# A depthwise 7x7 convolution as sixteen 32x32 tiles of TensorE, with rows cut into halves and columns into residues of four

## The chip, the core and the metric

The kernel runs on one core of one Trainium2 chip. The metric is the device time in microseconds (us) of one execution. TensorE (PE, with weight loads shown as PEld), VectorE (DVE), ScalarE (ACT) and GpSimd (POOL) compute; SyncE (SP) only issues transfers (DMA), which ScalarE and GpSimd can do as well. The core's transfers are carried out by 16 DMA engines.

## What is computed

A ConvNeXt block and a selective scan, in float32, on x of shape (32, 96, 56, 56):

```
h = depthwise 7x7 convolution of x (padding 3) + conv_b
h = (h - mean over channels) * rsqrt(var + eps) * ln_g + ln_b
h = gelu(h @ w1 + b1) @ w2 + b2           # 96 -> 384 -> 96, at every pixel
x = h * layer_scale + x
x = silu(depthwise 5x5 convolution of x + conv_b)
dts, Bs, Cs = x_proj_w @ x                # 6, 4 and 4 rows
delta = softplus(dt_w @ dts + dt_b)
P = exp(cumsum(max(delta * A, log eps)))  # over the 3136 tokens of an image
hs = P * cumsum(delta * Bs * x / max(P, eps))
y = sum over n of hs * Cs + x * Ds
```

A depthwise convolution mixes only pixels of one channel. On TensorE it becomes a product with a band matrix: input rows stand on the partitions, the weights hold the seven vertical taps of one horizontal tap, and one matmul is needed for each horizontal tap (or group of them).

## The kernel before, in words

The host lays x out as [96 channels, 112 rows, 896 columns]: 112 rows are two groups of images by 56 rows, 896 columns are 16 images by 56. Four stages follow one another, each through tensors in device memory (`conv1_d`, `block_d`, `conv2_d`, `du_d`).

**First convolution** (lines 141 to 363). A job is one channel: 80 jobs have both image groups, and the last 16 channels are done as 32 jobs of one group each, so that the first group's sums are ready early. For each job SP loads x by groups of 56 rows (`load_x`, L160) and the weights by two transfers (`taps_of`, L314, from a table written once, L184). Then the columns are split into even and odd by copies (L328 on POOL and DVE, L329 on ACT) into `xq`, the odd ones on partitions 0 to 55, the even ones on 64 to 119. That puts two horizontal taps into one contraction of 120 rows, so four matmuls with 448 columns do seven taps (L334; each is two passes, that is two matmul instructions and two weight loads). ACT evicts with the bias (L343), POOL issues the stores to `conv1_d` (L347), and DVE and ACT collect the sums for the norm over channels: difference to channel 0 (L356), its sum (L357), its square (ACT, L358), the sum of squares (L359). The preparation of the other stages' weights (`beside`) runs between jobs. `finish_norm` turns the sums of one image group into `rstd_d`.

**MLP** (L369 to L485). 28 groups of four rows. `load_rows` loads for each group the reciprocal deviation `r` (L394), three blocks of 32 channels of `h` (L399) with four rows named as the outermost dimension, and three of `x` (L404, 32 channels by one row in a transfer). DVE normalises (L411), TensorE multiplies by w1 in four row tiles (L421), ACT applies Gelu (L431), TensorE multiplies by w2 in four column tiles (L440), DVE adds the bias and x (L451, twice for each result), and POOL issues the stores to `block_d` (L463).

**Second convolution** (L492 to L579). One channel at a time: weights (L510), 120 rows by 1920 B twice (L521), four column tiles of TensorE (L533), Silu (L547), copies that interleave the columns (L556), a store of 28 rows (L562).

**Scan** (L587 to L810). 64 steps of 1568 tokens, 192 units of 32 channels by 4 states. SP loads `xs` (L621), TensorE and ACT make delta (L638, L646), POOL its product with x (L652), SP stores both (L655) and loads them spread over the states (L695). ACT makes the decay (L701 to L703), POOL multiplies by B (L707), DVE scans (L717, L720, L724), POOL multiplies by C (L735), TensorE sums over the states (L748), ACT copies and stores (L758, L759).

Instructions run on each engine in the order in which the program has them, after a scheduler has arranged what isn't pinned (`pin`). SP issues its transfers in that order too, waiting where a buffer isn't free. The lines that the change and the prediction's steps touch:

Of the kernel before, what the change touches and what calls it, by code (L numbers as in the profile page):

```python
# [15 lines left out]
B2, BI = 2, 16  # L16
# [7 lines left out]
WP = 128  # L24
W2 = W // 2
MP = 64
P1 = (K1 + 1) // 2
# [3 lines left out]
RW = 32  # L31
QP = QW + 1
# [6 lines left out]
EPS = 1e-9  # L39
APART = 16  # L40
# [7 lines left out]
def convnext_then_scan_kernel(  # L48
# [30 lines left out]
    conv1_d = dram.tile([C, ROWS, COLS], F32, name="conv1_d")  # L79
# [3 lines left out]
    rstd_d = dram.tile([ROWS, COLS], F32, name="rstd_d")  # L83
    taps1_d = dram.tile([C, 3 * WP * P1], F32, name="taps1_d")
# [21 lines left out]

    KR = MP + H
    PQ = HALF

# [11 lines left out]
    first = stats.tile([ROWS, B2, HALF], F32, name="first")  # L121
    acc1 = stats.tile([ROWS, B2, HALF], F32, name="acc1")
    acc2 = stats.tile([ROWS, B2, HALF], F32, name="acc2")
    sq = stats.tile([ROWS, B2, HALF], F32, name="sq")

    def finish_norm(j):

        a1, a2 = acc1[:, j], acc2[:, j]
        nc.vector.tensor_mul(sq[:, j], a1, a1)
        nc.vector.scalar_tensor_tensor(  # L130
            a2, in0=sq[:, j], scalar=-1.0 / C, in1=a2, op0=ALU.mult, op1=ALU.add
        )
        nc.vector.tensor_scalar(a2, a2, 1.0 / C, 0.0, ALU.mult, ALU.max)
        nc.scalar.activation(a2, a2, AF.Sqrt, bias=eps_t[:ROWS], scale=1.0)
        nc.vector.reciprocal(a1, a2)
        for s in range(2):
            nc.gpsimd.dma_start(
                rstd_d[j * H : (j + 1) * H, s * PQ : (s + 1) * PQ], a1[s * H : (s + 1) * H]
            )

    with tc.tile_pool(name="c1", bufs=3) as pool, tc.tile_pool(
        name="c1k", bufs=1
    ) as keep, tc.tile_pool(name="prep", bufs=1) as prep, tc.tile_pool(
        name="c1_ps", bufs=4, space=PSUM
    ) as psum:
        wts = [keep.tile([128, 2, H * P1], F32, name=f"wt1_{i}") for i in range(5)]
        xqs = [keep.tile([128, B2, BI, W2 + 3], F32, name=f"xq_{i}") for i in range(3)]
        jobs = [(c, (0, B2)) for c in range(C - APART)]
        jobs += [(c, (j, j + 1)) for j in range(B2) for c in range(C - APART, C)]
# [4 lines left out]
        xts: dict = {}  # L154

        def load_x(n):
# [18 lines left out]
        c1b_t = across(c1b, ROWS, C, "c1b_t", const)  # L175
        pad = prep.tile([C, 3, WP, P1], F32, name="pad1")
        nc.vector.memset(pad, 0.0)
        at = H - 1 - K1 // 2
        for i in range(3):
            for t in range(P1):  # L180
                j = 2 * t + 1 - i
                if j in range(K1):
                    nc.vector.tensor_copy(pad[:, i, at : at + K1, t], kt1[:, :, j])
        nc.sync.dma_start(taps1_d, pad.rearrange("c d p t -> c (d p t)"))  # L184
        for t in wts + xqs + [acc1, acc2]:
            nc.vector.memset(t, 0.0)
# [119 lines left out]
        def taps_of(n):  # L306

            c, wt = jobs[n][0], wts[n % len(wts)]
            for s in range(2):
                taps = bass.AP(  # L310
                    taps1_d.tensor, taps1_d.offset + (c * 3 + 1 - s) * WP * P1,
                    [[P1, H], [WP * P1, 2], [1, H * P1]],
                )
                nc.sync.dma_start(wt[MP * s : MP * s + H], taps)  # L314

        for n in range(4):
            taps_of(n)
        for n, (c, js) in enumerate(jobs):
            if n + 4 < len(jobs):
                taps_of(n + 4)  # L320
            if n + 2 < len(jobs):
                load_x(n + 2)

            xq, xt = xqs[n % len(xqs)], xts.pop(n)
            for j in range(*js):
                xv = xt[MP * j : MP * j + H].rearrange("p (i r s) -> p s i r", i=BI, s=2)
                copy = nc.vector.tensor_copy if j else nc.gpsimd.tensor_copy
                copy(xq[:H, j, :, 2 : W2 + 2], xv[:, 1])  # L328
                nc.scalar.copy(xq[MP:KR, j, :, 1 : W2 + 1], xv[:, 0])  # L329
            wv = wts[n % len(wts)].rearrange("p o m -> p (o m)").rearrange("p (q t) -> p t q", t=P1)  # L330
            ps = bank(f"ps1_{n}")[:ROWS, :, :PQ]
            for t in range(P1):
                for j in range(*js):
                    nc.tensor.matmul(  # L334
                        ps[:, j].rearrange("p (i r) -> p i r", i=BI),
                        lhsT=wv[:KR, t],
                        rhs=xq[:KR, j, :, t : t + W2],
                        start=(t == 0),
                        stop=(t == P1 - 1),
                    )  # L340
            half = slice(*js)
            ht = pool.tile([ROWS, B2, HALF], F32, name=f"ht_{n}", tag="ht") if c else first
            nc.scalar.activation(  # L343
                ht[:, half], ps[:, half], AF.Identity, bias=c1b_t[:, c : c + 1], scale=1.0
            )
            for s in range(2):
                nc.gpsimd.dma_start(  # L347
                    conv1_d[c, js[0] * H : js[1] * H, s * PQ : (s + 1) * PQ].rearrange(
                        "(j m) q -> m j q", m=H
                    ),  # L350
                    ht[s * H : (s + 1) * H, half],
                )
            if c:

                dt = pool.tile([ROWS, B2, HALF], F32, name=f"dt_{n}", tag="dt")
                nc.vector.tensor_sub(dt[:, half], ht[:, half], first[:, half])  # L356
                nc.vector.tensor_add(acc1[:, half], acc1[:, half], dt[:, half])  # L357
                nc.scalar.activation(dt[:, half], dt[:, half], AF.Square)  # L358
                nc.vector.tensor_add(acc2[:, half], acc2[:, half], dt[:, half])  # L359
            if n >= 3 and beside:  # L360
                beside.pop(0)()
            if n == C + 1:
                finish_norm(0)
# [5 lines left out]
    with tc.tile_pool(name="mlp_ot", bufs=1) as pool_o, tc.tile_pool(  # L369
        name="mlp_g", bufs=14  # L370
    ) as pool_g, tc.tile_pool(name="mlp", bufs=2) as pool, tc.tile_pool(
        name="mlp_h", bufs=3, space=PSUM
    ) as ps_h, tc.tile_pool(name="mlp_o", bufs=2, space=PSUM) as ps_o:
        blocks = C // CB
        rts: dict = {}
        hts: dict = {}
# [4 lines left out]
            pool_o.tile([128, QC, BI, QP], F32, name=f"o_{i}") for i in range(2 * blocks)  # L381
# [4 lines left out]
        def rows_of(d, row, b):  # L386
            return d[CB * b : CB * b + CB, row : row + RB, :].rearrange("c r q -> r c q")

        def load_rows(n):
            row = n * RB  # L390
            j, m = divmod(row, H)
            rt = pool.tile([128, COLS], F32, name=f"r_{n}", tag="r", bufs=3)
            rts[n] = rt
            nc.sync.dma_start(  # L394
                rt, bass.AP(rstd_d.tensor, rstd_d.offset + row * COLS, [[COLS, RB], [0, CB], [1, COLS]])
            )
            for d in range(blocks):
                ht = pool.tile([128, COLS], F32, name=f"h_{n}_{d}", tag="h", bufs=9)
                nc.sync.dma_start(ht, rows_of(conv1_d, row, d))  # L399
                hts[n, d] = ht  # L400
            for d in range(blocks):
                xt = pool.tile([128, COLS], F32, name=f"x_{n}_{d}", tag="x", bufs=9)
                for i in range(RB):
                    nc.sync.dma_start(  # L404
                        xt[CB * i : CB * i + CB],
                        x[CB * d : CB * d + CB, j * H + H - 1 - m - i, :],
                    )
                xts[n, d] = xt

        def normalise(n, d):  # L410
            pin(nc.vector.tensor_mul(hts[n, d], hts[n, d], rts[n]))  # L411
# [24 lines left out]
        def result(n, s, d):  # L436
# [11 lines left out]
            ot = ots[(n * blocks + d) % len(ots)]  # L448

            for e in range(2):  # L450
                pin(nc.vector.scalar_tensor_tensor(  # L451
                    ot[:, 2 * e + s, :, e : e + QW],
                    in0=po[:, :HALF].rearrange("p (i a e) -> p e i a", i=BI, e=2)[:, e],
                    scalar=b2r_t[:, d : d + 1],
# [16 lines left out]
        for d in range(blocks):  # L471
            normalise(0, d)
        for k in range(parts + 1):
# [3 lines left out]
            if k == 3:  # L477
                finish_norm(1)
# [376 lines left out]
```

## Time and profile before

| | us |
|---|---|
| median of 3 runs | 3618.1 (3617.41 to 3619.6) |
| the profiled execution, its time | 3618.94 |
| the profiled execution, its span | 3617.1 |
| first matmul of the first convolution (L334) | 17.9 |
| first matmul of the MLP (L421) | 612.3 |
| first matmul of the second convolution (L533) | 1469.5 |
| first matmul of the scan stage (L638) | 1827.0 |

The profile gives for each engine its busy time in 40 equal slices of the span, in tenths; for groups of equal instructions their number, the time in which at least one ran, the mean time of one, the idle time of the engine just before them and what ended it; and for any stretch the busy time of each engine, the clock granted to TensorE, the mean busy share of the 16 DMA engines and the rate. Matmuls overlap, so one's own time is longer than the distance between two. A share of a mean over the whole span says little here, since the four stages have different limits; each is read by itself.

### The profile page before, as it was taken

The numbers are of one execution on the slowest core, as the hardware profiler recorded it, in microseconds if no ns is written. First come the engines' busy times: TensorE is split into PE (matmuls) and PEld (weight loads), VectorE is DVE, ScalarE is ACT, GpSimd is POOL, SyncE is SP. The second block draws the span as 40 slices with busy tenths as digits, with TensorE's granted clock in tenths as the row PEclk, the third lists the DMA queues.
The fourth block names the chain that finished last, engine by engine and source line by source line (L and its number), as shares of the span: only waits on it lengthen the run. The fifth ranks groups of instructions, "written<-read, shape, count | busy, mean of one in ns | idle before, by whom it ended". The sixth has DMA issues, their size and how long they took to land. (4 is left out here: it accounts for less than half of the span.)

```text
span 3617.1 us, 46656 instructions
## 1 busy us (share of the span) xinstructions
PE 3051.3 (84%) x17290; PEld 1285.1 (36%) x17290; DVE 2659.5 (74%) x1816; ACT 2347.6 (65%) x2166; POOL 1973.9 (55%) x1286
## 2 busy tenths in 40 slices
PE   8999998999999999899848777777777778777775
PEld 5777775333333333333312222222222222222221
DVE  6666666333333333799949999999999999999998
ACT  4555554333333333588758888887888887888884
POOL 2333343222222222000048899998999998999996
PEclk9999999999999999999956667666667666767666
DMA  6655555444444542799977877877877877877873
GB/s 184 194 179 167 172 171 168 157 158 159 157 160 158 158 157 81 220 283 286 276 237 247 279 257 262 286 260 257 282 255 261 288 257 252 287 250 268 286 255 110
DMA packets 307052, 793.92 MB, mean 219 GB/s; under 512 B 124089, under 2 KB 185553, under 8 KB 282153
## 3 DMA queue, kind: packets, MB, share of 16 engines
q1 hardware_dynamic: 260176, 671.66, 57.6%
q0 software_dynamic: 29632, 80.27, 7.1%
q10 hardware_dynamic: 17016, 39.01, 2.9%
q8 instruction: 137, 2.24, 0.3%
q14 instruction: 91, 0.74, 0.1%
HBM read 555.05 MB, written 235.74 MB: 219 GB/s over the span
## 5 line engine op out<-in xcount | busy, mean ns | idle before, releaser
L735 POOL TENSOR_TENSOR hs<-hs,ct 128x1568 f32<-128x1568 f32 x192 | 672.9, 3504 | 106.1 <-DVE hs L724 96.8
L717 DVE TENSOR_TENSOR_SCAN pv<-rep,pv 128x1568 f32<-128x1568 f32 x192 | 664.5, 3461 | 73.3 <-ACT rep L703 56.0
L707 POOL TENSOR_TENSOR rep<-rep,bt 128x1568 f32<-128x1568 f32 x192 | 674.4, 3513 | 15.3 <-DMA rep<-du_d 15.3
L431 ACT ACTIVATE g<-ph,b1p_t 128x896 f32<-128x896 f32 x336 | 320.4, 1005 | 511.6 <-PE ph L421 511.5
L451 DVE SCALAR_TENSOR_TENSOR o<-po,b2r_t,x 128x224 f32<-128x224 f32 x336 | 190.6, 608 | 568.1 <-PE po L440 568.1
L334 PE MATMUL ps<-xq,wt 120*112 120x448 f32 x1536 | 582.9, 540 | 20.2 <-DMA wt<-taps_d 17.9
L463 POOL DMA_DIRECT2D block_d<-o x336 | 183.1, 552 | 659.2 <-DVE o L451 625.2
L334 PEld LDWEIGHTS ps<-xq,wt 120*112 120x112 f32 x1536 | 428.7, 280 | 172.7 <-issue 20.2
L421 PE MATMUL ph<-h,w1r_t 32*128 32x448 f32 x4032 | 438.2, 558 | 24.7 <-DVE h L411 22.6
L652 POOL TENSOR_TENSOR du<-du,xs 96x784 f32<-96x784 f32 x128 | 236.1, 1846 | 372.4 <-ACT du L646 372.4
L638 PE MATMUL pz<-xs,wd_t 96*96 96x392 f32 x512 | 276.5, 705 | 173.2 <-ACT du L646 137.6
L440 PE MATMUL po<-g,w_t 128*32 128x448 f32 x4032 | 413.0, 543 | 0.0
L748 PE MATMUL py<-hs,sel_t 128*32 128x392 f32 x1536 | 328.2, 684 | 72.2 <-POOL hs L735 72.2
L683 PE MATMUL pk<-bn,pick_t 8*128 8x392 f32 x1024 | 288.9, 684 | 100.2 <-ACT y L758 81.2
L720 DVE SCALAR_TENSOR_TENSOR pv<-pv,rep 128x1568 f32<-128x1568 f32 x192 | 345.6, 1800 | 21.1 <-POOL hs L735 1.4
L533 PE MATMUL ps<-xq,wt 128*32 128x448 f32 x3072 | 308.7, 547 | 41.8 <-DMA xq<-block_d 39.8
L724 DVE TENSOR_TENSOR_SCAN hs<-rep,carry_h,pv 128x1568 f32<-128x1568 f32 x96 | 334.0, 3480 | 10.8 <-PE pk L683 0.5
L556 DVE COPY st<-yt 28x896 f32<-28x896 f32 x288 | 317.2, 1101 | 33.0 <-ACT yt L547 14.4
L724 DVE TENSOR_TENSOR_SCAN hs<-rep,pv 128x1568 f32<-128x1568 f32 x96 | 328.4, 3421 | 9.9 <-DVE pv L720 0.5
L701 ACT ACTIVATE rep<-rep,a_t 128x1568 f32<-128x1568 f32 x192 | 308.4, 1606 | 13.5 <-DMA rep<-du_d 13.1
L702 ACT ACTIVATE rep<-rep,lift_t 128x1568 f32<-128x1568 f32 x192 | 307.7, 1602 | 6.2
L703 ACT ACTIVATE rep<-rep,lift_t 128x1568 f32<-128x1568 f32 x192 | 307.6, 1602 | 6.3
(84 smaller groups left out, 3188.3 us busy)
## 6 DMA issues: line engine op xcount, KB each, us to landing
rep<-du_d SPq DMA_DIRECT2D x192, 1568.0 KB
du_d<-du SPq DMA_DIRECT2D x128, 588.0 KB
xq<-block_d SPq DMA_DIRECT2D x192, 225.0 KB
block_d<-o POOLq DMA_DIRECT2D x336, 120.0 KB, 5.8
xt<-in_x_dram SPq DMA_DIRECT2D x192, 196.0 KB
x<-in_x_dram SPq DMA_DIRECT2D x336, 112.0 KB
h<-conv_d SPq DMA_DIRECT2D x84, 448.0 KB
conv_d<-st SPq DMA_DIRECT2D x96, 392.0 KB
```

What stands on the lines that cost most here:

```text
L334: nc.tensor.matmul(ps[:, j].rearrange("p (i r) -> p i r", i=BI), lhsT=wv[:KR, t], rhs=xq[:KR, j, :, t : t + W2], start=(t == 0), stop=(t = ...
L421: pin(nc.tensor.matmul(phs[i // 2][:, i % 2, :HALF], lhsT=w1r_t[rows, d, f * 128 : (f + 1) * 128], rhs=hts[n, d][rows, s * HALF : (s + 1) ...
L431: nc.scalar.activation(gt, ph[:, :, :HALF], AF.Gelu, bias=b1p_t[:, f : f + 1], scale=1.0)
L440: pin(nc.tensor.matmul(po[CB * i : CB * i + CB, :HALF], lhsT=w2_t[:, f, CB * d : CB * d + CB], rhs=gts[n, s, f, i // 2][:, i % 2], start=( ...
L533: pin(nc.tensor.matmul(ps[RW * f : RW * f + RW, h, : B * QW].rearrange("p (b q) -> p b q", q=QW), lhsT=wv[:, f, t], rhs=xv[:, :, t : t + Q ...
L556: pin(copy(st[:, :, :, :, f], yt[RW * f : RW * f + QR].rearrange("p h (b q) -> p h b q", q=QW),))
L707: pin(nc.gpsimd.tensor_mul(ut, ut, bts[i // NG]))
L717: pin(nc.vector.tensor_tensor_scan(grown, da, zero, pv[:, last : last + 1] if q else 1.0 / EPS, ALU.mult, ALU.add))
L720: pin(nc.vector.scalar_tensor_tensor(run, in0=grown, scalar=1.0, in1=ut, op0=ALU.min, op1=ALU.mult))
L724: pin(nc.vector.tensor_tensor_scan(ht, da, run, carry_h[:, col : col + 1] if q else 0.0, ALU.mult, ALU.add))
L735: pin(nc.gpsimd.tensor_mul(ht, ht, cts[k]))
L748: pin(nc.tensor.matmul(py[g * DG : (g + 1) * DG, s, :BK], lhsT=sel_t, rhs=hss[k * NG + g][:, cols], start=False, stop=True, tile_position= ...
```

## The change

In the first convolution a job is now four pieces: for 80 channels two channels by two halves of rows (an upper and a lower half of 28 output rows each, which need 31 input rows), for the last 16 channels four channels by one half. The four pieces stand on partitions 0, 32, 64 and 96. Output columns are split by their residue mod 4, one residue for each column tile of TensorE, so that a matmul is a 32x32 tile with 31 rows of contraction and up to 448 columns; a job has 7 taps by 4 residues by 4 pieces, 112 matmuls. The input is read from the loaded tile in steps of four columns, and there are no copies. Each job loads four pieces of x and four of taps. The stores go from POOL's queue to ScalarE's. The sums are collected for four pieces at a time.

`conv1_d` and `rstd_d` are ordered by half, row, residue and column, and the MLP takes its groups in that order: four rows and two residues at a time, with `x` loaded once for two groups and one operation instead of two for a result. Its first loads stand before the end of the first convolution.

In the scan, the first step's work is ordered anew: delta is stored and spread before its product with x, which DVE makes there. The last unit's product with C is split between DVE and POOL, and the last sum over states takes two of its three parts earlier.

```diff
+R1 = QR + K1 // 2
+TP = R1 + K1 // 2 + RW
+JT = 4
...
-    conv1_d = dram.tile([C, ROWS, COLS], F32, name="conv1_d")
+    conv1_d = dram.tile([C, 2, QR, QC, HALF], F32, name="conv1_d")
...
+        jobs = [[(c, 0), (c, 1), (c + 1, 0), (c + 1, 1)] for c in range(0, C - APART, 2)]
+        whole = len(jobs)
+        jobs += [
+            [(c + k, h) for k in range(JT)] for h in range(2) for c in range(C - APART, C, JT)
+        ]
...
         def load_x(n):
-            c, js = jobs[n]
-            xts[n] = pool.tile([128, COLS], F32, name=f"xt1_{n}", tag="xt")
-            for j in range(*js):
-                nc.sync.dma_start(xts[n][MP * j : MP * j + H], x[c, j * H : (j + 1) * H])
+            xts[n] = pool.tile([128, 2 * COLS], F32, name=f"xt1_{n}", tag="xt")
+            for k, (c, h) in enumerate(jobs[n]):
+                nc.sync.dma_start(
+                    two(xts[n][RW * k : RW * k + R1]),
+                    x[c].rearrange("(j m) q -> m j q", m=H)[h * (H - R1) : h * (H - R1) + R1],
+                )
...
+        def load_taps(n):
+            wt = pool.tile([128, RW * K1], F32, name=f"wt1_{n}", tag="wt")
+            for k, (c, h) in enumerate(jobs[n]):
+                at = taps1_d[c, (1 - h) * (K1 // 2) * K1 : (1 - h) * (K1 // 2) * K1 + 1]
+                nc.sync.dma_start(
+                    wt[RW * k : RW * k + R1],
+                    bass.AP(at.tensor, at.offset, [[K1, R1], [1, RW * K1]]),
                 )
...
+        def convolve(n):
+            wv = wts.pop(n).rearrange("p (o j) -> p j o", j=K1)
+            xv = xts.pop(n).rearrange("p (b q f) -> p f b q", q=QW, f=QC)
+            pss = [bank(f"ps1_{n}_{a}") for a in range(JT // 2)]
+            order = sorted(range(K1), key=lambda j: j != K1 // 2)
+            for j in order:
+                for f in range(QC):
+                    far, g = divmod(f + j - K1 // 2, QC)
+                    lo, hi = max(0, -far), QW - max(0, far)
+                    for k in range(JT):
+                        rows = slice(RW * k, RW * k + R1)
+                        nc.tensor.matmul(
+                            pss[k // 2][RW * f : RW * f + RW, k % 2, :HALF].rearrange(
+                                "p (b q) -> p b q", q=QW
+                            )[:, :, lo:hi],
+                            lhsT=wv[rows, j],
+                            rhs=xv[rows, g, :, lo + far : hi + far],
+                            start=(j == order[0]),
+                            stop=(j == order[-1]),
+                            tile_position=(RW * k, RW * f),
+                        )
...
+                nc.scalar.dma_start(to, hs[RW * f : RW * f + QR])
...
+        for n in range(len(jobs)):
+            if n + 3 < len(jobs):
+                load_taps(n + 3)
+                load_x(n + 3)
+            pss = convolve(n)
+            if n == whole + len(jobs[whole:]) // 2:
+                finish_norm(0)
+            hs = evict(n, pss)
...
+            add_sums(n, hs)
...
+            if n == len(jobs) - 3:
+                load_rows(0)
+                load_rows(1)
+            if n == len(jobs) - 2:
+                for d in range(blocks):
+                    normalise(0, d)
...
-            for e in range(2):
-                pin(nc.vector.scalar_tensor_tensor(
-                    ot[:, 2 * e + s, :, e : e + QW],
+            pin(nc.vector.scalar_tensor_tensor(
+                ot[:, f].rearrange("p (b r) -> p b r", r=QP)[:, :, at : at + QW],
...
+            if p == 0 and at == 0:
+                deltas, products = slice(0, 1), slice(1, 2)
+                warm = pool.tile([C, 1], F32, name="warm", bufs=1)
+                pin(nc.scalar.activation(warm, dtb_t, AF.Softplus))
+                for h in range(2):
+                    delta_in(0, h)
+                for h in range(2):
+                    delta(0, h)
+                for h in range(2):
+                    keep_du(0, h, deltas)
+                spread_du(0, deltas)
+                for h in range(2):
+                    delta_x(0, h, nc.vector)
+                    keep_du(0, h, products)
...
+            if i < units - 1:
+                pin(nc.gpsimd.tensor_mul(ht, ht, cts[k]))
+            else:
+                for engine, cols in (nc.vector, slice(0, HT)), (nc.gpsimd, slice(HT, CH)):
+                    pin(engine.tensor_mul(ht[:, cols], ht[:, cols], cts[k][:, cols]))
```

More of the change, by code (lines that the diff above doesn't have):

```diff
@@ L23 @@
 K1, K2 = 7, 5
[L24 to L27, printed above, removed]
 QC = 4
@@ L120, in convnext_then_scan_kernel @@
     stats = front.enter_context(tc.tile_pool(name="stats", bufs=1))
[L121 to L129, printed above, removed]
+    acc1 = stats.tile([128, 2, 2, HALF], F32, name="acc1")
+    acc2 = stats.tile([128, 2, 2, HALF], F32, name="acc2")
@@ L135, in finish_norm @@
         nc.vector.reciprocal(a1, a2)
-        for s in range(2):
-            nc.gpsimd.dma_start(
-                rstd_d[j * H : (j + 1) * H, s * PQ : (s + 1) * PQ], a1[s * H : (s + 1) * H]
-            )
[L141 to L149, printed above, removed]
+        for f in range(QC):
+            nc.gpsimd.dma_start(rstd_d[h, :, f], a1[RW * f : RW * f + QR])
@@ new lines, in evict @@
+        def evict(n, pss):
+            job = jobs[n]
+            hs = (
+                pool_o.tile([128, JT, HALF], F32, name=f"hs1_{n}", tag="hs")
+                if n
+                else pool_o.tile([128, JT, HALF], F32, name="first", bufs=1)
+            )
+            step = 2 if n < whole else 1
+            for k in range(0, JT, step):
+                c = job[k][0]
+                nc.scalar.activation(
+                    hs[:, k : k + step],
+                    pss[k // 2][:, k % 2 : k % 2 + step, :HALF],
+                    AF.Identity,
+                    bias=c1b_t[:, c : c + 1],
+                    scale=1.0,
+                )
+            c, h = job[0]
+            for f in range(QC):
+                if n < whole:
+                    to = conv1_d[c : c + 2, :, :, f].rearrange("a h m q -> m (a h) q")
+                else:
+                    to = conv1_d[c : c + JT, h, :, f].rearrange("a m q -> m a q")
+                nc.scalar.dma_start(to, hs[RW * f : RW * f + QR])
+            return hs
@@ new lines, in add_sums @@
+        def add_sums(n, hs):
+            dt = pool_o.tile([128, JT, HALF], F32, name=f"dt_{n}", tag="dt", bufs=2)
+            h = jobs[n][0][1]
+            if n < whole:
+                base = first[:, :2].rearrange("p (o h) q -> p o h q", o=1).to_broadcast(
+                    [128, 2, 2, HALF]
+                )
+                parts = [(slice(0, JT), acc1, acc2)]
+                nc.vector.tensor_sub(
+                    dt.rearrange("p (a h) q -> p a h q", h=2),
+                    hs.rearrange("p (a h) q -> p a h q", h=2),
+                    base,
+                )
+                flat = lambda t: t.rearrange("p (a h) q -> p a h q", h=2)
+            else:
+                base = first[:, h : h + 1].to_broadcast([128, JT, HALF])
+                parts = [(slice(a, a + 2), acc1[:, :, h], acc2[:, :, h]) for a in (0, 2)]
+                nc.vector.tensor_sub(dt, hs, base)
+                flat = lambda t: t
+            for ks, a1, _ in parts:
+                nc.vector.tensor_add(a1, a1, flat(dt[:, ks]))
+            nc.scalar.activation(dt, dt, AF.Square)
+            for ks, _, a2 in parts:
+                nc.vector.tensor_add(a2, a2, flat(dt[:, ks]))
@@ L380, in convnext_then_scan_kernel @@
         ots = [
-            pool_o.tile([128, QC, BI, QP], F32, name=f"o_{i}") for i in range(2 * blocks)
+            pool_o.tile([128, QC, B * QP], F32, name=f"o_{i}") for i in range(2 * blocks - 1)
         ]
@@ L810, in convnext_then_scan_kernel @@
                 gather(after, 1)
+            if i == units - 1:
+                for h in range(2):
+                    gather(steps - 1, h, range(NG - 1))
+            if i == units:
+                for h in range(2):
+                    gather(steps - 1, h, range(NG - 1, NG))
+                store(steps - 1, 0)
+                store(steps - 1, 1, nc.vector.tensor_copy, nc.sync)
 def kernel(**inputs):
```

296 lines of the change are left out of this document (148 added, 148 removed).

## The prediction, made before the changed kernel ran

> **What bounds the kernel now.** I read the page first (its slices show four stages), then the busy time by stretches, the groups of lines inside the first stage, and the DMA view of chosen stretches. From the page, and below it the groups of the stretch from 40 to 560 us, inside the first convolution:
>
> ```profile
> PE   8999998999999999899848777777777778777775
> DVE  6666666333333333799949999999999999999998
> ```
> ```profile
> L334 PE MATMUL ps<-xq,wt 120*112 120x448 f32 x1376 | 519.5, 538 | 0.0
> L359 DVE TENSOR_TENSOR acc<-acc,dt 112x896 f32<-112x896 f32 x78 | 86.1, 1104 | 80.9 <-ACT dt L358 80.9
> L356 DVE TENSOR_TENSOR dt<-ht,first 112x896 f32<-112x896 f32 x78 | 85.2, 1092 | 54.9 <-ACT ht L343 54.5
> L357 DVE TENSOR_TENSOR acc<-acc,dt 112x896 f32<-112x896 f32 x78 | 85.1, 1092 | 2.6
> L358 ACT ACTIVATE dt<-dt 112x896 f32<-112x896 f32 x78 | 74.1, 950 | 134.0 <-DVE acc L357 134.0
> ```
> The first stage is TensorE's: no idle time before L334 (last column 0.0). Its 1376 matmul instructions took 520 us, so one starts every 0.378 us (the 538 ns is one's length, overlapping the next). The stage runs from 0 to the first matmul of the MLP (L421) at 612.3 us in the timeline. The MLP, to about 1458, is TensorE's as well; the second convolution, to about 1815, is bound by transfers (DMA share 0.93); the scan by VectorE and GpSimd. So what the change does to the first stage counts in full, provided nothing else becomes the bound there. That is the question, and two stretches outside this stage answer it:
>
> ```profile
> core 0: us, PE busy (x) PEld busy (x) DVE busy (x) ACT busy (x) POOL busy (x), PEclk, DMA share, GB/s
> 40.00:560.00 520.00, 520.00 (x1386) 385.23 (x1385) 327.56 (x380) 275.36 (x359) 172.98 (x280) 1.00 0.58 179
> 1000.00:1008.00 8.00, 7.46 (x76) 2.76 (x72) 3.27 (x5) 2.44 (x3) 0.00 (x0) 1.00 0.25 97
> 1500.00:1780.00 280.00, 254.24 (x2540) 109.08 (x2536) 264.66 (x239) 223.96 (x159) 0.00 (x0) 1.00 0.93 283
> ```
> From 1000 to 1008 us only loads of `h` (L399) and `r` (L394) are in flight: three of 448 KB, issued from 997 to 999 us, and a fourth at 1003. Yet the share is 0.25: four engines of sixteen, 97 GB/s together, 24 per engine. These loads name their rows four at a time (outermost dimension 4, "r c q"). The three don't use twelve engines; they queue on the same four.
>
> The DMA view of the second convolution lets the engines be counted:
>
> ```profile
> DMA packets 38369, 79.22 MB, mean 283 GB/s; under 512 B 4752, under 2 KB 33885, under 8 KB 38340
> xq<-block_d SPq DMA_DIRECT2D x160, 225.0 KB
> conv_d<-st SPq DMA_DIRECT2D x79, 392.0 KB
> wt<-taps_d SPq DMA_DIRECT2D x79, 128.0 KB
> ```
> The packets under 512 B are 4 bytes each: one ends the share of each engine in a transfer. If 120 rows go to 15 engines, 28 to 14 and 128 to 16, there should be 160x15 + 79x14 + 79x16 = 4770; there are 4752. In all transfers issued by SP, then, every engine takes an equal number of rows, with at most 16 engines: 8 of 120, 2 of 28, 8 of 128, 4 of 56, 1 of 4.
>
> **The change, part by part.**
>
> *Loads of the first convolution.* Each of 48 jobs (40 whole, 8 half) loads four pieces of x and four of taps, all of 31 rows. 31 is prime: equal shares mean one engine with 31 rows or 31 engines, and there are 16. No transfer of the trace has such a number, so the bounds are wide: one engine from above, sixteen from below (the nearest row in size is the load of 32 rows, L404, on sixteen). I take one engine, because every count above is an equal share, and because the loads that use few engines share the same ones, so that all eight of a job queue on one.
> The Trainium skill, page "DMA: Bandwidth & Descriptors", section "Why a DMA increments its semaphore by 16 and not by 1", says the same against this change: the count is the largest up to 16 that divides the outermost dimension of both sides, and a transfer of 127 partitions uses one engine. By that rule the sum is the one below; by a rule of shares rounded up, which the counts here also fit, 31 rows would go to sixteen, and the sum is that of the first rival.
>
> What one engine then has to do, from the packet records of the trace:
> - x: 48 x 4 x 31 x 2 = 11,904 packets of 3584 B. In the MLP 28 of these start per us on four engines when these run alone, 143 ns each: 1702 us. (140 ns, their median length, gives 1667; the 24 GB/s of the stretch above, 150 ns, gives 1786.)
> - taps: 48 x 4 x 31 = 5952 of 896 B. Their median is 41 ns, their mean 54, and 1024 B take 46; I take 45: 268 us (244 to 321).
> - its part of the stores (28 rows, so 14 engines, 8 packets of 1792 B at 74 ns, 48 x 4 times): 114 us.
> - `r` and `h` of the MLP's first two groups, 2 x 128 packets: 37 us.
>
> Sum 2121 us, 43 us a job. Add 3 before the first packet, 3 in which SP waits for the table of taps (its write stands behind the first x loads on that engine), and 10 for the last job's matmuls. The first matmul of the MLP then comes at 2137 us in place of 612.3: **+1525 us**.
>
> *What that hides.* TensorE per job: 112 matmuls in two passes, 224 instructions; with sixteen tiles at once 14 x 0.375 = 5.3 us; at half clock, which the idle stretches of the scan bring (PEclk 0.53 to 0.69), 10. VectorE: three operations on 1792 elements; 624 ns for 448 and 1092 for 896 give 2.02 each, 6.05 us, and up to 1.8 more of waiting for Square (today 1.04 for a Square of 0.95). ScalarE: two evictions of 1.01, a Square of 1.7 and four issues, moved here from POOL's queue, at 0.32 to 0.45 us: 5.5 us. All lie inside 43 us, with three jobs of loads ahead, and cost nothing; without that cover the largest of them is the job (first rival). The removed copies (L328, L329) and POOL's issues (L347) waited for TensorE and save nothing. On SP's queue only the first loads of the MLP stand behind these, and I counted them; on ScalarE's queue the new issues stand ahead of Square, inside the 5.5 us.
>
> The matmul reads every fourth element of x. No matmul of the trace does; bounds are 5.3 and 10.5 us a job (VectorE's L451, which reads so, takes 608 ns for 224 elements, L130 624 for 448). Both are under 43. The Trainium skill, page "SBUF — State Buffer", gives the reason why it may cost: lines of 16 bytes need two hits for full rate, and every fourth float is a line of its own; by it the job is 10.5 us, still hidden.
>
> *MLP.* The 8064 matmul instructions are the same and are the bound. L451 goes from 336 of 608 ns to 168 of twice the size (0.63 to 1.22 us each, 106 to 205 us in all, 204 before) while VectorE waited 568 us for `po`; `x` and `block_d` go in half as many transfers with the same bytes. 0, between -10 and +10 for the first group.
>
> *Scan.* At the start, xs lands at 1827.0 and the first scan (L717) starts at 1859.7. Delta alone is now stored and spread first: Softplus to about 1831, store 1834, half of the 7.9 us that the first `rep` took, decay 4.8 us: about 1844, 15 us earlier (10 to 25, as the second unit's extra 7 us may go too). At the end, the last weighing (3.48 us) is split and two thirds of the last gather stand ahead of it: 6 us (3 to 7). Together -21.
>
> **Sum.** The profiled execution took 3618.94 us (span 3617.1), 0.8 above the median of 3618.1. 2137 + (3618.9 - 612.3) - 21 = 5123; I say **5120**. Ends: 1667 + 244 + 114 + 37 + 16, and -30 for the scan, give 5055; 1786 + 321 + 114 + 37 + 16, and -10, give 5271. A little overlap of packets on one engine is possible (more than 16 packets at a time are seen, up to 20), so 5030 to 5270.
>
> **Rivals.**
> *Loads spread over many engines (the other side).* If 31 rows go to sixteen engines, a job's loads take 43/16 = 2.7 us and VectorE is the bound: 6.05 to 7.85 us a job, 290 to 377, and 40 for the start and the weights' preparation: the MLP starts at about 370, total 370 + 3006.6 - 21 = **3356** (3310; 3510 if strided reads double TensorE's time to 10.5 us). It decides by the number of engines: the stage before cost 612.3/48 = 12.7 us per such job, so from 43/12.7 = 3.4, that is four engines, the change is faster. For it: sixteen in the load of 32 rows. Against it: no unequal share in any count.
> *Four tiles at a time.* The change may not do what it says: the trace shows four tiles at once (in the MLP four matmuls start between 1001.333 and 1001.353 us, the next at 1001.709) and never more. If TensorE keeps only four busy, 10,752 instructions at 94 ns are 1011 us, and if the loads spread, the MLP starts at 1030: **4016**. With the loads on one engine this is hidden too.
>
> **How the numbers follow.** One engine 0.86, spread 0.10, spread but four tiles 0.04. The range 5030 to 5270 holds the first case 93 times in 100, so 0.80 in all. Faster by over 0.2% (about what a measurement of this kernel tells from no change) 0.10, within 0.2% 0.01 (what the spread cases leave between the signs), slower 0.89.
>
> **What would show it.** Right: DMA share about 0.1 and some 30 GB/s in the first stage, TensorE idle before its matmuls with the loads of `xt` and `wt` named as releasers, jobs 43 us apart, L421's successor first at about 2140 us, the scan's stage some 20 us shorter. Wrong: a share above 0.4 there, or a conv stage under 1000 us; then the loads are spread, and the wait before the third VectorE operation decides the time.

## The result, and the profile after

The changed kernel takes **5011.2 us** (median of 4 runs, 5010.34 to 5015.82), the kernel before in the same comparison 3617.8: a ratio of 1.3853 (95% 1.3832 to 1.3874), slower. The profiled execution took 5010.34 us, its span is 5008.6. The forecast was 5120, from 5030 to 5270: the direction and the mechanism are right, the time lies 19 us under the range.

The page's slices, to be laid beside those of before (TensorE, VectorE, then the granted clock, the share of the DMA engines and the rate):

```profile
PE   2333333333333332899999989777777778777776
...
DVE  1111111111111111422333389789999999999999
...
PEclk9666666666666666999999999866666666676676
DMA  0111111111111112544444399888878777877874
GB/s 30 49 45 46 46 45 47 45 44 45 44 47 44 45 44 68 152 157 155 154 153 156 108 274 288 251 288 267 275 258 270 267 268 256 278 274 251 275 273 159
```

The first sixteen slices (125 us each) are the first convolution. TensorE is busy a third of the time, VectorE a tenth, the transfers a tenth or two, at 45 GB/s: nobody is busy, by a view that averages sixteen DMA engines. The same for the stretch from 500 to 1500 us by the view of windows, and what was waited for:

```profile
core 0: us, PE busy (x) PEld busy (x) DVE busy (x) ACT busy (x) POOL busy (x), PEclk, DMA share, GB/s
500.00:1500.00 1000.00, 335.58 (x5575) 208.19 (x5562) 146.01 (x74) 83.74 (x72) 0.00 (x0) 0.66 0.15 45
```
```profile
engine line waited for: us in total, times, longest us
ACT dt L415 <- DMA conv_d<-hs: 905.3, 24, 41.8
DVE acc L417 <- ACT dt L415: 844.5, 24, 39.3
PEld ps L355 <- ACT hs L377: 715.1, 48, 33.3
PE ps L355 <- ACT hs L377: 664.2, 24, 31.8
```

In 1000 us 24.5 jobs were done, one every 40.85 us. The waits seem to accuse ScalarE: Square (L415) waits for the stores, VectorE for Square, TensorE for the eviction (L377). No line names the loads. The timeline of ScalarE for one job shows why: in 41 us it computes for 3.6 and stands 37 in four DMA issues (the line "ACTq"; the columns are start and duration in us, engine, line, operation, and in brackets the idle time before).

```profile
1030.00 1.70 ACT L415 ACTIVATE dt<-dt 128x1792 f32<-128x1792 f32 x1 [37.42 <-DMA conv_d<-hs]
1031.60 1.89 ACT L377 ACTIVATE hs<-ps,c1b_t 128x896 f32<-128x896 f32 x2
1033.52 37.21 ACTq L390 DMA_DIRECT2D conv_d<-hs  x4
```

So there are two readings of one profile, and both fit the waits: the stores' issues hold ScalarE and so the stage, or the loads hold an engine and the issues are one more thing that stands behind it. The packet records of the trace speak for the second. From 991.7 to 1073.4 us (two jobs) the loads' packets follow one another without a gap over 0.1 us:

```
packets of two jobs          count   mean ns   distance of starts ns
x, 3584 B                      496         140   136.5 (207 now and then)
taps, 896 B                    248          41   37.7
stores, 1792 B (14 engines)    896         121
```

248 x 136.5 + 124 x 37.7 ns is 38.5 us; the x packets that start later than 136.5 ns, all beside stores, add 2.27 us a job, which is 71 ns for each of the 32 store packets that a fourteenth part of 448 puts on that engine. Sum 40.8: one engine's row of packets is the job. Behind the first convolution the stages are as before: from the first matmul of the MLP to the end of the span 2983.5 us, before 3004.8.

### The profile page after: what moved, and what is told of

The parts are those of the page before. It is cut to its first block, busy times and chain, and to the rows that moved or that the text cites. A ratio compares the mean times of both kernels' runs of the same rounds, so it can differ in the third digit from the quotient of the medians.

```text
span 5008.6 us, 62478 instructions
## 1 busy us (share of the span) xinstructions
PE 3120.8 (62%) x26506; PEld 1266.2 (25%) x26506; DVE 2570.6 (51%) x1370; ACT 2215.3 (44%) x1915; POOL 1678.1 (34%) x799
## 5 line engine op out<-in xcount | busy, mean ns | idle before, releaser
L355 PE MATMUL ps<-xt,wt 31*32 31x448 f32 (+1 forms) x10752 | 652.3, 962 | 1297.9 <-ACT hs L377 1166.2
L417 DVE TENSOR_TENSOR acc<-acc,dt 128x1792 f32<-128x1792 f32 (+1 forms) x56 | 98.5, 1759 | 1621.4 <-ACT dt L415 1621.1
L415 ACT ACTIVATE dt<-dt 128x1792 f32<-128x1792 f32 x48 | 81.4, 1696 | 1756.5 <-DMA conv_d<-hs 1554.0
L355 PEld LDWEIGHTS ps<-xt,wt 31*32 31x32 f32 x10752 | 409.9, 144 | 1536.2 <-ACT hs L377 1254.4
L513 DVE SCALAR_TENSOR_TENSOR o<-po,b2r_t,x 128x448 f32<-128x448 f32 x168 | 170.9, 1017 | 579.2 <-PE po L500 551.8
L481 PE MATMUL ph<-h,w1r_t 32*128 32x448 f32 x4032 | 438.4, 559 | 30.9 <-DVE h L167 22.3
L788 DVE TENSOR_TENSOR_SCAN hs<-rep,carry_h,pv 128x1568 f32<-128x1568 f32 x96 | 334.1, 3480 | 10.4 <-DVE pv L784 0.5
L524 POOL DMA_DIRECT2D block_d<-o x168 | 81.2, 490 | 750.3 <-DVE o L513 587.7
```

Source lines behind the costliest of these rows:

```text
L355: nc.tensor.matmul(pss[k // 2][RW * f : RW * f + RW, k % 2, :HALF].rearrange("p (b q) -> p b q", q=QW)[:, :, lo:hi], lhsT=wv[rows, j], rhs ...
L481: pin(nc.tensor.matmul(phs[i // 2][:, i % 2, :HALF], lhsT=w1r_t[rows, d, f * 128 : (f + 1) * 128], rhs=hts[n, d][rows, s * HALF : (s + 1) ...
L788: pin(nc.vector.tensor_tensor_scan(ht, da, run, carry_h[:, col : col + 1] if q else 0.0, ALU.mult, ALU.add))
```

## Experiments

Theory A is the prediction's: 31 rows go to one DMA engine, and the sum of its packets is the stage. Rival B: the stores on ScalarE's queue hold it. The first four runs tell these apart, the others take up what they left.

**32 rows.** The extra row is one of x that meets weights of zero:

```diff
-R1 = QR + K1 // 2
+R1 = RW
-        nc.vector.tensor_copy(pad[:, QR - 1 : QR - 1 + K1], kt1)
+        nc.vector.tensor_copy(pad[:, QR : QR + K1], kt1)
-                at = taps1_d[c, (1 - h) * (K1 // 2) * K1 : ... + 1]
+                at = taps1_d[c, (1 - h) * QC * K1 : ... + 1]
```

> One change against the changed kernel: every load of x and of taps in the first convolution has 32 rows in place of 31 (the extra row meets weights of zero). Theory A, one engine: a transfer of 31 rows goes to a single DMA engine, and that engine's packets set the 40.85 us of a job; 32 rows go to sixteen, the engine is left with 2.4 us of loads a job, and the next bound is TensorE, 13.5 us a job at a granted clock of 0.67, about 9.0 at full clock. The MLP starts at about 490 us, the whole takes about 3480 us (3400 to 3600). Rival B, the stores: ScalarE stands 37 us of each job in the issues of the four stores, and eviction and TensorE wait behind it; the loads are only late with it. The stores are the same here, so a job stays near 40 us and the whole near 5000.

Measured: 3605.1 us, 0.9973 of before (0.9963 to 0.9982). One row more in each load, 3% more bytes, and 1406 us are gone. B falls: the stores are unchanged and ScalarE no longer stands. The window from 100 to 560 us:

```profile
core 0: us, PE busy (x) PEld busy (x) DVE busy (x) ACT busy (x) POOL busy (x), PEclk, DMA share, GB/s
100.00:560.00 460.00, 460.00 (x8684) 437.95 (x8673) 239.45 (x128) 140.05 (x123) 0.00 (x0) 1.00 0.56 160
```

TensorE is busy throughout, at full clock, and a job takes 11.87 us. The expected 3480 was too low: it scaled the job with the clock, from 13.5 us at 0.67 to 9.0 at 1.0. But 0.67 is a mean that takes in the idle time between jobs. While the matmuls of one job ran, the granted clock was 0.80 (538.1 to 551.7 us) or 0.91 (991.7 to 1005.4 us), and the job took 12.6 us from its first to its last start both times; the second and the fifth job of the changed kernel, at 1.00, took 11.9 and 12.4. So a job hardly follows the clock; what bounds it instead is taken up below.

**Only the taps with 32 rows**, x with 31:

```diff
-                    wt[RW * k : RW * k + R1],
-                    bass.AP(at.tensor, at.offset, [[K1, R1], [1, RW * K1]]),
+                    wt[RW * k : RW * k + RW],
+                    bass.AP(at.tensor, at.offset, [[K1, RW], [1, RW * K1]]),
```

> Only the loads of taps have 32 rows, x keeps 31. Theory A: 124 packets of 37.7 ns a job leave the one engine (4.7 us, 0.3 come back as its share of sixteen), so a job takes 36.4 us in place of 40.8 and the whole about 4805 us (4790 to 4830). Rival B: no change, 5011. If the time falls to that of the kernel with all loads at 32 rows, then it was the table of taps and not x.

Measured: 4811.1 us, 36.48 us a job. The taps' term of the sum is what A says (4.36 us less a job, 4.4 expected).

**Stores on POOL's queue**:

```diff
-                nc.scalar.dma_start(to, hs[RW * f : RW * f + QR])
+                nc.gpsimd.dma_start(to, hs[RW * f : RW * f + QR])
```

> The stores of the first convolution go back to POOL's queue, all else as in the changed kernel. Theory A: the engine's work is the same or loses at most the stores' 2.3 us a job (110 us); what goes besides is the 54 us for which ScalarE stood behind the loads of the MLP's first rows at the end of the stage, some 45 of it on the path: 4855 to 4970 us. Rival B: ScalarE is free, and a job takes what TensorE needs, at most 13.5 us: below 3750 us.

Measured: 4985.9 us, 40.5 us a job (40.2 and 40.7 in turn). B falls a second time, and the waits of this kernel are those that the prediction had looked for:

```profile
ACT hs L377 <- PE ps L355: 821.6, 25, 36.8
DVE dt L402 <- ACT hs L377: 818.6, 25, 36.7
PEld ps L355 <- issue: 690.6, 210, 10.5
PE ps L355 <- DMA xt<-in_x_dram: 544.7, 74, 9.0
```

ScalarE now waits for TensorE, and TensorE for the loads of x. The stall in the issues had covered the true releaser and cost next to nothing during the stage. A's own range is missed by 16 us: a store costs nearly as much from this queue (0.35 us a job less), and the end of the stage, from the last load of x to the first matmul of the MLP, shrinks from about 63 to 44 us, not by 45.

**Stores twice**, the second into a tensor that nobody reads:

```diff
+    spare_d = dram.tile([C, 2, QR, QC, HALF], F32, name="spare_d")
...
+                for there in conv1_d, spare_d:
...
+                    nc.scalar.dma_start(to, hs[RW * f : RW * f + QR])
```

> Each store of the first convolution is issued twice on ScalarE's queue, the second into a tensor that nobody reads. Theory A: 32 more packets a job on the busy engine, 71 ns each by the time that the loads' packets lose now beside stores: +2.3 us a job, 5120 us (5105 to 5140). If stores only fill gaps between the loads, 5011 to 5030. Rival B: the time in ScalarE's issues doubles, 6500 us or more.

Measured: 5149.6 us, 43.65 us a job: 2.8 us for 32 more packets, 88 ns each, a little above the 71 read from the trace. Stores do not slip into gaps: the prediction was right to count them.

**What bounds the kernel with 32 rows?** Its matmuls take 1.7 times as long as the MLP's (964 ns against 558 and 543). Read without the step of four columns, so that other columns are multiplied:

```diff
-            xv = xts.pop(n).rearrange("p (b q f) -> p f b q", q=QW, f=QC)
+            xv = xts.pop(n).rearrange("p (f b q) -> p f b q", q=QW, f=QC)
```

> As the kernel with 32 rows, but TensorE reads 14 neighbouring columns at a time (every group of 448 is a contiguous quarter of the loaded row) in place of every fourth; the sorting of the columns by residue is left out, so other numbers are computed by as many instructions of the same sizes. With 32 rows a job takes 11.87 us of TensorE, 53 ns from one matmul instruction to the next at full clock and 950 to 1000 ns for each, where sixteen tiles at the MLP's 0.375 us would give 23 ns and 5.3 us. Theory S, the strided reading: it costs TensorE its rate; without it a job takes 6 to 8 us (VectorE's 6.05 and its waits, or the transfers), the whole 3335 to 3430 us. Rival D, the issue: 224 matmuls and 224 weight loads a job go through TensorE at 26.5 ns each whatever they read: 3605 us, no change.

Measured: 3469.7 us, 0.9597 of before (0.9583 to 0.9611); 8.6 us a job. The groups of TensorE from 100 to 400 us, first with 32 rows and strided, then contiguous:

```profile
line engine op names shapes xcount | busy us, mean ns | idle before us <-releasers
L355 PE MATMUL ps<-xt,wt 32*32 32x448 f32 (+1 forms) x5653 | 301.4, 964 | 0.0
```
```profile
line engine op names shapes xcount | busy us, mean ns | idle before us <-releasers
L355 PE MATMUL ps<-xt,wt 32*32 32x448 f32 (+1 forms) x7778 | 255.1, 556 | 45.6 <-issue 43.1 <-DVE wd_t L303 2.2
```

D is wrong, and S is right that the step costs TensorE its rate: one matmul falls from 964 to 556 ns, the busy time per instruction from 53.3 (301.4 / 5653) to 32.8 ns (255.1 / 7778). S's own figures are missed, the job by 0.6 us and the whole by 40: 32.8 is not the 23 of sixteen tiles at the MLP's rate, and the job is not held by TensorE any more (255 of 300 us).

The weights are read with a step too, of seven:

```diff
-            wv = wts.pop(n).rearrange("p (o j) -> p j o", j=K1)
+            wv = wts.pop(n).rearrange("p (j o) -> p j o", j=K1)
```

> As the contiguous kernel, and the weights of a matmul are read as 32 neighbouring numbers in place of every seventh (other numbers again, as many instructions). There a matmul starts every 31 to 32 us/1000 (7.1 us a job when TensorE is busy), which is 506 ns for each of sixteen tiles; the MLP's 375 ns and the 141 ns of a weight load add up to 516. Theory W: on a tile the weight load and the matmul follow one another, and the load's own time counts; the MLP's loads from neighbouring numbers take 109 ns, so 484 ns a tile, 30.3 ns a matmul, 6.8 us a job. Rival: the weight loads lie beside the matmuls; their time may fall, the distance of the matmuls stays at 31 to 32 ns. The whole changes little in both cases, 3440 to 3475 us.

Measured (one run): 3465.5 us. A weight load falls from 141 to 104 ns; TensorE is busy 249.4 us for 7729 instructions, 32.3 ns each. W expected 30.3: it gets about a fifth of that. What keeps sixteen tiles from 23 ns stays open.

**Sorting by copies.** POOL copies each residue into a tile of its own ahead of the matmuls:

```diff
+            xq = pool.tile([128, 2 * COLS], F32, name=f"xq1_{n}", tag="xq", bufs=2)
+            xv = xq.rearrange("p (f b q) -> p f b q", q=QW, f=QC)
+            for f in range(QC):
+                nc.gpsimd.tensor_copy(xv[:, f], xs[:, f])
```

> As the kernel with 32 rows, but POOL, which is idle there, first sorts the columns by residue into a second tile (four copies of 448 columns a job, 0.62 us each by the copies of the kernel before), and TensorE reads that tile in runs of 14. Theory S: as the contiguous kernel and some 3 us for the first job: 3340 to 3440 us, faster than both kernels by 5 to 8 in 100. Rival D: 3605 to 3610. If POOL's copies become the bound: they are 2.5 us a job, so not unless they take over 12.

Measured: 3523.6 us, 0.9749 of before (0.9733 to 0.9766): half of what was expected. The next run moves the copies to ScalarE, one job ahead, the stores to POOL's queue, and gives Square a tile of its own:

```diff
+            for f in range(QC):
+                nc.scalar.copy(xv[:, f], xs[:, f])
...
-                nc.scalar.dma_start(to, hs[RW * f : RW * f + QR])
+                nc.gpsimd.dma_start(to, hs[RW * f : RW * f + QR])
...
-            nc.scalar.activation(dt, dt, AF.Square)
+            st = pool_o.tile([128, JT, HALF], F32, name=f"st_{n}", tag="st", bufs=2)
+            nc.scalar.activation(st, dt, AF.Square)
```

> As the kernel with 32 rows, with three more edits: ScalarE (not POOL) sorts the columns by residue, one job ahead; the stores go back to POOL's queue; Square writes a tile of its own, so that it can run beside VectorE's second operation. Theory C, contention: POOL's copies took 1.95 us each where they had taken 0.62, and VectorE's operations 2.5 to 2.9 us where they take 2.02 alone, so the two engines took time from each other; on ScalarE the copies cost 2.4 us a job, ScalarE has 6.1 us a job in all, VectorE 6.05, TensorE 7.1, and a job takes 7.1 to 8.0 us: 3405 to 3450 us. Rival T, the transfers: a job moves 1.8 MB, which at the 216 GB/s of the contiguous kernel is 8.3 us; then 3465 to 3485 us, and VectorE's operations are at 2.02 us all the same. If VectorE stays at 2.5 us and more, C is wrong.

Measured: **3438.4 us, 0.951 of before (0.9497 to 0.9523)**, the fastest version here. The VectorE sum L418 and POOL's copies in the first, the same sum (L423) and ScalarE's copies in the second:

```profile
L348 POOL COPY xq<-xt 128x448 f32<-128x448 f32 x120 | 227.3, 1950 | 74.5 <-issue 73.9 <-POOL xq L348 0.6
...
L418 DVE TENSOR_TENSOR acc<-acc,dt 128x1792 f32<-128x1792 f32 x30 | 86.4, 2878 | 1.0
```
```profile
L349 ACT COPY xq<-xt 128x448 f32<-128x448 f32 x144 | 144.8, 1117 | 0.0
...
L423 DVE TENSOR_TENSOR acc<-acc,dt 128x1792 f32<-128x1792 f32 x33 | 66.8, 2025 | 1.1
```

C is right about the engines: beside POOL's copies the same VectorE operation took 2878 ns, beside ScalarE's 2025, as in the kernel with 32 rows and no copies (2025); a POOL copy with no VectorE operation beside it took 0.96 to 1.1 us (7 of 192), their mean in the stage 1950. The Trainium skill, page "SBUF — State Buffer", section "SBUF: two separate sides", gives the reason: VectorE (with two inputs) and GpSimd share one pair of ports, and the one that comes second waits; the two kernels agree with it.

About the job C is wrong: 8.4 us, not 7.1 to 8.0. T's 8.3 fits, but T is not shown:

```profile
core 0: us, PE busy (x) PEld busy (x) DVE busy (x) ACT busy (x) POOL busy (x), PEclk, DMA share, GB/s
100.00:400.00 300.00, 259.57 (x7984) 176.82 (x7970) 217.40 (x114) 264.41 (x257) 83.11 (x144) 0.99 0.90 225
```

The DMA engines are busy 0.90 of the time (0.76 in the contiguous kernel), but ScalarE is busy 0.88 and TensorE 0.87, and ScalarE has 7.4 us a job (264 us for 35.6 jobs), not C's 6.1. No run here takes these apart. That the whole fell into C's range all the same, and under T's, goes mostly with the end of the stage: in the contiguous kernel, with the stores on ScalarE's queue, the last job started 29 us after the one before it, here 8 us. The run made three edits at once and doesn't say what each brought to the whole.

**Is it the number of rows?** Two runs with one transfer cut into two. In the kernel with 32 rows, x in 17 and 15 rows:

```diff
+                for a, b in (0, 17), (17, R1):
                     nc.sync.dma_start(
-                        two(xts[n][RW * k : RW * k + R1]),
+                        two(xts[n][RW * k + a : RW * k + b]),
```

> As the kernel with 32 rows, but each load of x is cut into 17 rows and 15 rows: the same bytes and the same tile. Theory A, the number of engines is a divisor of the number of rows: 17 is prime and over 16, so it goes to one engine, 15 to fifteen. That engine then has 4 x 2 x 17 packets of x at 136.5 ns (18.6 us), 1.1 us of the rest, 0.3 of taps and 2.3 of stores a job, 22.3 us in place of TensorE's 11.87: 3605 + 47 x 10.4 = 4094 us (4060 to 4130). Rival, shares rounded up (31 rows would have been an exception of its own): 3605 to 3620.

And the changed kernel, still with 31 rows, with x and taps in 16 and 15:

```diff
+                for a, b in (0, 16), (16, R1):
...
-                        two(xts[n][RW * k : RW * k + R1]),
+                        two(xts[n][RW * k + a : RW * k + b]),
...
-                    wt[RW * k : RW * k + R1],
+                        wt[RW * k + a : RW * k + b],
```

> The changed kernel with its 31 rows, the same bytes, no extra row, but every load of x and of taps is cut into 16 rows and 15 rows. Theory A: sixteen and fifteen engines, so the first has 2 rows of 31 in place of all; SP issues 16 transfers a job, about 8 us at 0.5 us each, under TensorE's 11.87 us: 3605 to 3625 us. If it were 32-row transfers alone that spread, or the odd number of bytes in a table that slows, the time would stay at 5011 or fall only in part.

Measured: 4264.6 us (25.9 us a job) and 3867.8 us (18.1 us a job from 250 to 550 us, not the 17.4 of the expectation below). The first rival is out, and 31 rows do spread when cut in two, but both are slower than A's sums. In the second TensorE counted as busy without a pause (300 of 300 us) with only 3715 matmuls, where the kernel with 32 rows had 5653:

```profile
core 0: us, PE busy (x) PEld busy (x) DVE busy (x) ACT busy (x) POOL busy (x), PEclk, DMA share, GB/s
250.00:550.00 300.00, 300.00 (x3715) 225.80 (x3706) 101.80 (x51) 61.30 (x51) 0.00 (x0) 1.00 0.50 104
```

The suspect is the order of the instructions: with more transfers per tile the scheduler had sorted the matmuls by piece, so that fewer tiles worked at once (12 matmuls in flight, not 18). In the next two runs the matmuls of both kernels are kept in the written order:

```diff
-                        nc.tensor.matmul(
+                        pin(nc.tensor.matmul(
```

> As the kernel with loads of 16 and 15 rows, but TensorE's matmuls are kept in the order in which the program writes them. There the scheduler had put the matmuls of one piece behind one another, so that about eleven instead of seventeen or eighteen were in flight (12.7 starts per us at 965 ns each) and a job took 17.4 us. Theory O, the order: with the written order a job takes 11.9 us again and the whole 3605 to 3625 us. Rival, the loads: sixteen transfers a job in place of eight (and packets of 308 ns) hold the job at 17 us whatever the order: 3860 us.

> As the kernel with x in 17 and 15 rows, with the matmuls kept in the written order, since there too the scheduler had sorted them by piece. Theory A says 22.3 us a job from the one engine's packets, and 25.9 were measured: if the order was what lengthened it, 22.3 to 23.5 us a job and 4095 to 4155 us in all. If the one engine simply takes 25.9 us for its packets, 4265 us stays.

Measured: 3688.9 us (13.6 us a job) and 4211.9 us (24.2 us a job). The first in the same stretch:

```profile
250.00:550.00 300.00, 295.72 (x4927) 203.21 (x4896) 133.70 (x66) 79.49 (x68) 0.00 (x0) 0.97 0.65 135
```

The order was 4.5 of the 6.2 us over 11.87 in the first. The other 1.7 go with SP, whose issues now follow one another almost without a pause, sixteen a job, 0.8 us each where 0.5 was taken. Whether these issues are the bound, or themselves stand behind busy DMA engines as ScalarE's did, no run here tells:

```profile
586.60 8.95 SPq L340 DMA_DIRECT2D wt<-taps_d  x8
595.60 3.60 SPq L188 DMA_DIRECT2D xt<-in_x_dram  x8
599.29 9.56 SPq L340 DMA_DIRECT2D wt<-taps_d  x8
```

In the second, 22.3 had been expected: 1.7 of the excess went with the order, 1.9 stays. Of that some 0.6 us is in the starts of the lone packets (most of them 140 to 146 ns apart, not 136.5); the rest is not settled. All four kernels with cut loads also have an MLP that is 24 to 31 us longer than the changed kernel's, for which no cause was looked for. That 17 rows go to one engine, as equal shares have it, is shown; the price of that engine's packets is some 8% above the sum.

## Why the prediction was right and wrong

**One engine for 31 rows: right**, by the packets, by 32 rows, by 17 rows and by 16 and 15.

**What one engine needs: the step that failed.** "In the MLP 28 of these start per us on four engines when these run alone, 143 ns each: 1702 us", and 45 ns for the taps:

| | forecast us | measured us |
|---|---|---|
| start and table | 6 | 3 (first packet of x; no gap at the table) |
| x, 11,904 packets | 143 ns: 1702 | 136.5 ns: 1625 |
| taps, 5952 packets | 45 ns: 268 | 37.7 ns: 224 |
| stores | 114 | 47 jobs x 2.27: 107 |
| first rows of the MLP, last job | 47 | 64 (from about 1961) |
| first matmul of the MLP | 2137 | sum 2023, seen 2025.1 |

The starts were counted over whole microseconds (25 to 30 in each), pauses between packets included; that gave 143. In the same stretch of the kernel before, from 1000 to 1008 us, the distance to the fourth packet after (one engine of four) has a lower quartile of 137 ns, a median of 139 and a mean of 147: the figure of a full queue could have been read there. The low end of the range was no better: it took a packet's own length (140, 41) as the least distance, and in a full queue the next one starts 3.5 ns before the last ends. The 121 us too many for x and taps are more than the whole error of 109; the end of the stage took back 17.

**What it hides: right in sum, wrong in its parts.** ScalarE's issues, counted at 0.32 to 0.45 us each, took 37 us a job; TensorE's job took 13.5 us (at a granted clock of 0.8 to 0.9 while it ran), not 5.3 to 10.5. All of it still lay inside 40.85. The signs named were half right: the jobs were 40.85 us apart, not 43; the share was 0.15 and not 0.1, 45 GB/s and not 30, because the stores had been left out of that figure; the loads were named as releasers only once the stores had left ScalarE.

**Rivals.** Spread loads give 3605, not 3356: TensorE, not VectorE, is the next bound, at 11.87 us a job. So even the side of the forecast that was right about 32 rows was 250 us too hopeful (its bounds, added up again from its terms, are 3316 and 3530, not 3310 and 3510). Four tiles at a time is wrong: 5653 matmuls of 964 ns in 301 us are 18 in flight. The Trainium skill's 16-byte lines, of which two hits each are needed for full bandwidth (page "SBUF — State Buffer", section "Specifications (TRN2)"), point the right way. The factor of 2 was the prediction's own reading of them: the stride costs TensorE a factor of 1.6 (53.3 against 32.8 ns), and from a higher floor.

**MLP and scan.** -21.3 after the first matmul of the MLP against -21, but not from the steps named alone: the start of the scan (its first matmul to the first scan) 32.7 to 18.9 us (-13.8, forecast -15), the end 14.4 to 9.2 (-5.2, forecast -6); the MLP +2.9, the scans between +4.5, and the second convolution, which was not changed, 9.8 us shorter in this execution (357.6 to 347.7) and 4 to 8 in the other kernels with uncut loads. The two steps are confirmed, the exact sum is luck.

## What to carry to other kernels

Before a tile height is chosen, look at how many equal shares its rows make: 31 or 17 rows put a whole transfer on one of sixteen DMA engines, and a row of padding (or two transfers) gives the others back. A mean DMA share of 0.15 can be one engine that never rests; then the waits name whoever issues transfers, and only moving that issuer, or the packet records, shows the engine behind it. And a layout that feeds more tiles is worth what its reading costs: here the step of four columns ate most of what sixteen tiles gave, and with the columns sorted on ScalarE and the stores on POOL's queue the kernel came out 5% faster than before.

## What the runs showed of the hardware

- Packets of one queue on one engine start closer together than they are long (136.5 for 140 ns, 37.7 for 41), and a store's packet of 1792 B among them costs 71 to 88 ns.
- While one DMA engine was full, the instructions that issue transfers from ScalarE stood: four stores took 37 us, though the mean share of the sixteen engines was 0.15; on POOL's queue the same four took 2.3 us, and on ScalarE's with loads of 16 and 15 rows 2.4 to 2.9.
- A job on sixteen tiles, reading with a step of four, took 12.6 us from its first to its last matmul's start at a granted clock of 0.80 and of 0.91, and 11.9 and 12.4 at 1.00 (all with 31 rows): the time hardly followed the clock.
- Copies of 448 elements with a step of four took ScalarE 1.1 us here; with a step of two, on 56 partitions, 0.61 in the kernel before.
